# A four-layer graph network: layer 3's sums by accumulating DMAs, row spreads through DRAM, a new preparation

## The chip, the cores and the metric

The kernel runs on one NeuronCore of a Trainium2 chip. The time is device microseconds of one execution; the median of three runs is given. Engines: TensorE (PE, matrix products and transposes), VectorE (DVE), ScalarE (ACT), GpSimd (POOL), SyncE (SP, which issues DMAs; GpSimd and ScalarE can issue DMAs too). SBUF is the working memory of 128 partitions, PSUM the 8 banks that TensorE writes.

## The reference

32 samples of 512 nodes with 256 features pass through four layers; each adds its result to `x`. All share one 512 x 512 adjacency matrix `adj`. Everything is float32.

```python
h = max(layernorm(x), 0)                       # ahead of each layer
# layer 0: masked attention, 4 heads of 64
scores = q k^T / 8;  attn = softmax(where(adj == 0, -inf, scores));  x += concat(attn v) wo^T + bo
# layer 1: two graph attentions (GAT); the first without a mask, 512 features; the second masked, 256 features
gat(inp) = elu(softmax_j(leaky_relu(f1[i] + f2[j])) @ (inp W))
out = relu(h W1 + b1); out = elu(gat(out)) + out; out = relu(out W2 + b2); out = elu(gat(out)) + out; x += relu(out)
# layer 2: GAT with 4 heads of 64, masked;  x += elu(softmax_j(leaky(e_src[i] + e_dst[j])) @ q)
# layer 3: GAT with 8 heads of 32, masked, with beta*log(adj + 1e-6) added to the scores;  x += concat(...) W_out^T
```

The softmax is divided out late: the kernel forms the numerators `exp(score) * mask` for a block of 128 keys by 512 queries, multiplies them by the values, forms the sums over the keys apart, and divides afterwards.

## The kernel before, in words

**Preparation.** Lines 404 to 600 load the weights and `adj`, transpose `adj`, build the masks (`mask0T`, `mask1T`, `mask1`, `mask3T`), fold the attention vectors into the weight matrices (`w2`, `w3`, `fr1a`, `wh`) and compute a flag `go`, which says whether scores are small enough for the fast path. `go` is read by every engine as a branch; only the fast path, `pipelined`, runs here. `general` is the other branch. Preparation uses its own pool, `prep`; the tiles of `pipelined` come from the pool `big`, which takes the same memory once `prep` is freed.

**The planner.** `pipelined` writes no instruction directly. Each call through `q` is recorded as a step with an engine, a cost (function `cost`), the tiles it touches and its predecessors. When all 32 samples are recorded, `Plan.order` builds one order for all engines: it takes the step with the earliest start, and among those the one with the smallest due time. Due times come from `PERIOD` and the length of the chain behind a step, moved by `URGENT` for named tiles of a layer; `STARTS`, `PACE` and `LAYERS` hold samples and layers back. The steps are then issued in that order from line 261, so every operation of the pipeline has line 261 in the profile and is told apart by its tiles. Several samples are in flight, and each engine and each DMA queue runs its own part of the order strictly in sequence. The tiles of 128 x 512 share one tag, `block`, with `BLOCKS` buffers; PSUM tiles share the 8 banks.

**Units.** Products that use 32 or 64 columns (or 64 rows) of TensorE are issued in groups that fill the array; `unit("columns", ...)` or `unit("rows", ...)` marks such a group, with a packing mode that differs from full products.

**Layer 3 and layer 2** (`separable`, lines 889 to 943). Four heads at a time, the row `R[s]` of each head is spread over 128 partitions by a DMA from DRAM. For each of the 4 key blocks `j`, ScalarE and VectorE make four blocks `p` (one per head) and TensorE adds their products with the values to `av`. The sums over the keys are formed in two ways: in the first group of heads (`g == 0`; the only one of layer 2) VectorE adds the four `p` of each head into `total`, and TensorE multiplies the totals by ones at the end; in the second group of layer 3 TensorE multiplies every `p` by ones, into `sm`, in the same unit as `av`. Layer 3 then divides in `normalise` (lines 688 to 710): `sums` goes to DRAM, comes back as `few` (128 x 16), is inverted, goes to DRAM again, and comes back spread as `rc`. Layer 2 (lines 945 to 968) instead copies `av` and `sm` out as `y3`, transposes all three, and divides in node-major form.

**Layer 1** (`first_gat`, `second_gat`). The scores of the nodes come from the products `f1p`; a second product with `pick` brings them to node-major form. Three rows (`r1`, `rc`, `fb`) are spread over all partitions by four transposes each of a column broadcast to 128 x 128.

**The norm** (`norm_t`, lines 628 to 652) of every layer: statistics on VectorE, `rs` (a power of -0.5) on GpSimd, `h` on ScalarE, and eight transposes `pt` on TensorE.

Of the kernel before, what the change touches and what calls it, by code (L numbers as in the profile page):

```python
# [11 lines left out]
F32 = mybir.dt.float32  # L12
BF16 = mybir.dt.bfloat16
I32 = mybir.dt.int32
AF = mybir.ActivationFunctionType
# [15 lines left out]
G = 2  # L31
# [10 lines left out]
PERIOD = 51.0  # L42
STARTS, PACE = (0.0, 8.0, 36.0, 32.0), 110.0
LAYERS = (0.0, 51.0, 151.0, 201.0)

URGENT = {
    "stats:0": 76, "h:0": 358, "mm:0": 3, "sc:0": 60, "p0:0": -99, "av:0": 39, "stats:1": -269, "pt:1": 119,
    "nd:1": -201, "total:1": 12, "av:1": -22, "e:1": -39, "o2:1": 73, "s:1": -189, "pt:2": 15, "e4:2": -44,
    "total:2": 10, "stats:3": -38, "mv:3": -56, "mm:3": -12, "p3:3": -178, "total:3": -169, "sm:3": 86,
    "s1:3": -16,  # L50
}
BLOCKS, KEEP = 60, 2
KEEP_BANKS = 0
BANKS = ("mm", "av", "sm", "sc", "pt", "fb", "f1p")
# [242 lines left out]
def cost(engine, op, args, kw, out):  # L297
# [22 lines left out]
    if engine == "POOL":  # L320
        return (1.0 if n < 16 else 0.683), 0.1
    size = 4
    for _, k in (out.ap if out.tensor.name.startswith(("few", "R", "rc", "x")) else src.ap):
        size *= k
# [4 lines left out]
def gnn_stack_kernel(ctx: ExitStack, tc: tile.TileContext, a: dict, out: bass.AP):  # L329
# [29 lines left out]
    def load_col(name, eng):  # L359

        src = a[name]
        t = const.tile([P, src.shape[0] // P], F32, name=name)
        eng.dma_start(t, T(src, "(k p) -> p k", p=P))
        return t

# [19 lines left out]
    bq8 = const.tile([P, KD], F32, name="bq8")  # L385

# [6 lines left out]
    pick = const.tile([P, 2], F32, name="pick")  # L393
# [9 lines left out]

    prep_stack = ExitStack()
    prep = prep_stack.enter_context(tc.tile_pool(name="prep", bufs=2))
    pp = prep_stack.enter_context(tc.tile_pool(name="prep_psum", bufs=1, space=PSUM))
    with prep_stack, tc.manual_schedule():

        adj = prep.tile([P, NT, N], I32, name="adj", bufs=1)
        nc.gpsimd.dma_start(adj, T(a["adj"], "(t p) j -> p t j", p=P))  # L410
# [3 lines left out]
        nc.sync.dma_start(a2, bass.AP(tensor=src.tensor, offset=src.offset, ap=[[0, P], [1, 2 * F2]]))  # L414
        s3 = load_bcast(prep, "L3_a_src", nc.sync, D)
        d3 = load_bcast(prep, "L3_a_dst", nc.sync, D)
        wq = load_rows("wqT", nc.scalar, D)
        rows = []
        for name in ("bq", "bk"):
            t = prep.tile([1, D], F32, name=f"{name}r")  # L420
            nc.sync.dma_start(t, a[name][None, :])
            rows.append(t)
        for k in range(KD):
            nc.scalar.dma_start(
                T(w3[:, k, H3 : H3 + D], "p (h f) -> p h f", h=H3), T(a["L3_W"][:, k * P : (k + 1) * P, :], "h p f -> p h f")
            )
        wk = load_rows("wkT", nc.scalar, D)
        bt = load_bcast(prep, "beta", nc.sync, 1)
        bq = load_col("bq", nc.sync)
        bk = load_col("bk", nc.sync)  # L430
        afc = load_bcast(prep, "a_fc", nc.sync, 2 * HID)
        wo = load_rows("woT", nc.scalar, D)
        wv = load_rows("wvT", nc.scalar, D)
        wfc = load_rows("W_fc", nc.scalar, HID)
        bo = load_bcast(const, "bo", nc.sync, D)
        bv = load_bcast(const, "bv", nc.sync, D)
        bvc = prep.tile([P, KD], F32, name="bvc")
        nc.sync.dma_start(bvc, T(a["bv"], "(k p) -> p k", p=P))
        ahd = load_bcast(prep, "a_hand", nc.sync, 2 * D)
        b1 = load_col("mlp1_b", nc.sync)  # L440
        b2 = load_col("mlp2_b", nc.sync)
        wh = load_rows("W_hand", nc.scalar, D + 2)
        m1 = load_rows("mlp1_w", nc.scalar, HID)
        m2 = load_rows("mlp2_w", nc.scalar, D)
        w3o = load_rows("L3_WoT", nc.scalar, D)
# [10 lines left out]
        for c in range(2):  # L456
            nc.vector.tensor_reduce(pick[:, c : c + 1], ident[:, c:P:32], axis=AX.X, op=ALU.add)


        top = prep.tile([P, NT], F32, name="top")  # L460
        adjf = prep.tile([P, NT, N], F32, name="adjf", bufs=1)
        for t in range(NT):
            nc.vector.tensor_copy(adjf[:, t, :], adj[:, t, :])
        adjT = []
        for j in range(NT):
            pt = pp.tile([P, N], F32, name="adjT", bufs=NT)
            for t in range(NT):
                nc.tensor.transpose(pt[:, t * P : (t + 1) * P], adjf[:, t, j * P : (j + 1) * P], ident)
            adjT.append(pt)
        for t in range(NT):  # L470
            nc.vector.tensor_reduce(top[:, t : t + 1], adjf[:, t, :], axis=AX.X, op=ALU.max)
            nc.vector.tensor_scalar(mask1[:, t, :], adjf[:, t, :], 0.0, -BIG, op0=ALU.is_le, op1=ALU.mult)


        ab = prep.tile([P, 1], F32, name="ab")
        nc.vector.tensor_scalar(ab, bt, -1.0, None, op0=ALU.mult)
        nc.vector.tensor_tensor(ab, ab, bt, op=ALU.max)
        nc.scalar.activation(ab, ab, AF.Exp, scale=-1.0)
        m3 = [prep.tile([P, N], F32, name="m3", bufs=NT) for _ in range(NT)]
        for j in range(NT):  # L480
            nc.scalar.activation(m3[j], adjT[j], AF.Relu)
        nc.scalar.activation(ab, ab, AF.Ln, bias=one)

        ok = prep.tile([P, NT], F32, name="ok")
        nc.vector.tensor_scalar(ok, top, 0.0, None, op0=ALU.is_gt)
        nc.vector.tensor_scalar(top, top, 0.0, None, op0=ALU.max)
        nc.scalar.activation(top, top, AF.Ln, bias=eps)
        for j in range(NT):
            nc.scalar.activation(m3[j], m3[j], AF.Ln, bias=eps)
        nc.vector.scalar_tensor_tensor(beta, bt, 0.0, ab, op0=ALU.max, op1=ALU.add)  # L490

        for j in range(NT):
            nc.scalar.activation(m3[j], m3[j], AF.Exp, scale=beta)
# [9 lines left out]
        for w, h, f, vs, vd in (  # L503
            (w2, H2, F2, a2[:, 0:1, :].to_broadcast([P, H2, F2]), a2[:, 1:2, :].to_broadcast([P, H2, F2])),
            (w3, H3, F3, T(s3, "p (h f) -> p h f", h=H3), T(d3, "p (h f) -> p h f", h=H3)),
        ):
            project(lambda k: w[:, k, h : h + D], KD, h, f, vs, lambda k: w[:, k, :h])
            project(lambda k: w[:, k, h : h + D], KD, h, f, vd, lambda k: w[:, k, 3 * h + D :])
            nc.vector.tensor_scalar(w[:, :, h + D : 2 * h + D], w[:, :, :h], ALPHA - 1.0, None, op0=ALU.mult)
            nc.vector.tensor_scalar(w[:, :, 2 * h + D : 3 * h + D], w[:, :, 3 * h + D :], ALPHA, None, op0=ALU.mult)  # L510


# [3 lines left out]
        for w, row in zip((wq, wk), rows):  # L516
            gp = pp.tile([64, N], F32, name="gp", bufs=2)
            for h in range(4):
                c = slice(h * 64, (h + 1) * 64)
                for k in range(KD):  # L520
                    nc.tensor.matmul(gp[:, c], w[:, k, c], w[:, k, c], start=(k == 0), stop=False)
                nc.tensor.matmul(gp[:, c], row[:, c], row[:, c], start=False, stop=True)
# [10 lines left out]
        gab = prep.tile([64, D], F32, name="gab")  # L533
        nc.vector.tensor_copy(gab, gp[:, :D])
        nc.vector.tensor_tensor(gab, gab, gp[:, D:], op=ALU.mult)
        nc.vector.tensor_reduce(
# [865 lines left out]
```

## Time and profile before

| | |
|---|---|
| median of three runs | 4181.78 us (4181.32 to 4182.27) |
| the profiled execution's own time, and its span | 4184.13 us, 4182.3 us |
| TensorE busy | 4059.5 us, 97% |
| VectorE busy | 3312.1 us, 79% |
| ScalarE busy | 3004.7 us, 72% |
| GpSimd busy | 254.8 us, 6% |
| DMA moved | 181.07 MB; the hardware queue used 13.5% of 16 engines' span |
| granted TensorE clock, mean | 0.988 |
| additions into `total` (VectorE) | 832 and 416, 547.2 and 278.9 us |
| `sm<-p,ones` (TensorE, second group of layer 3) | 1024 records, 142.1 us |
| `y3` transposes (TensorE) | 384, 49.0 us |

A group's line gives the line and engine, the operation with the tiles written and read (buffer numbers left out), the shapes, the count, the busy time and the mean of one in ns, and after the bar the idle time of its engine just before it and what ended it. A timeline line gives the start, the duration, the engine, and how many like instructions were merged. The chain of work that ended last is followed back from the end of the execution. A float32 matrix product is two records, a transpose one. Durations of TensorE overlap; the distance of two starts is the time that one takes.

### The profile page before, as it was taken

What the parts mean: (1) busy time and instruction counts of PE and PEld (TensorE: products, weight loads), DVE (VectorE), ACT (ScalarE), POOL (GpSimd) and SP (SyncE); (2) the same over time, 40 slices, a digit from 0 to 9 for tenths busy, and PEclk for the clock granted to TensorE, in tenths of its full rate; (3) what the DMA queues carried; (4) which work ended last, traced back from release to release, by engine and by line L of the source; (5) the groups of instructions that cost most, each with busy time, mean ns of one, the idle gap of its engine ahead of it and who ended that gap; (6) DMA issues with size and microseconds to landing.
All of it is one profiled execution on the core that took longest, in us unless ns stands there. A gap on an engine that the chain in (4) does not pass through costs nothing.

```text
span 4182.3 us, 52787 instructions
## 1 busy us (share of the span) xinstructions
PE 4059.5 (97%) x17862; PEld 2068.7 (49%) x17862; DVE 3312.1 (79%) x7018; ACT 3004.7 (72%) x5970; POOL 254.8 (6%) x263
## 2 busy tenths in 40 slices
PE   5999999999999999999999999999999999999986
PEld 3545454554454554455554455554455554455442
DVE  5388877878877878877879877879877878877876
ACT  3467777766777766777766777776777776787774
POOL 1000000000000000000000000000000000000000
PEclk7999999999999999999999999999999999999998
DMA  2001111111110111110111111111111111111111
GB/s 84 11 21 47 47 47 33 49 52 32 47 51 30 49 52 32 47 52 30 49 52 32 47 52 31 47 52 32 47 52 32 46 52 32 47 52 32 41 42 52
DMA packets 149435, 181.07 MB, mean 43 GB/s; under 512 B 45858, under 2 KB 81572, under 8 KB 149156
## 3 DMA queue, kind: packets, MB, share of 16 engines
q1 hardware_dynamic: 143572, 172.37, 13.5%
q10 hardware_dynamic: 5312, 4.20, 0.3%
q8 instruction: 143, 2.34, 0.2%
q14 instruction: 136, 1.11, 0.1%
q0 software_dynamic: 272, 1.05, 0.1%
HBM read 158.41 MB, written 19.14 MB: 42 GB/s over the span
## 4 chain that ended last, share of the span: by engine, by line
PE 78%; DVE 13%; DMA 4%; ACT 2%; issue 1%; SPq 0%; POOL 0%; DVEq 0%; POOLq 0%
PE mm L261 36%; PE av L261 26%; PE pt L261 6%; PE sc L261 5%; PE sm L261 4%; DVE p L261 3%; DVE total L261 3%; DVE ue L261 2%; DMA rc<-s 2%; DVE o L261 2%; PE f1p L261 1%; DVE oT L261 1%; ACT p L261 1%; DVE x L261 1%; DMA s<-few 1%; DMA R<-rd 1%
## 5 line engine op out<-in xcount | busy, mean ns | idle before, releaser
L261 ACT ACTIVATE p<-R,e 128x512 f32<-128x512 f32 x1536 | 1010.2, 721 | 167.7 <-DMA R<-rd 167.5
L261 DVE SCALAR_TENSOR_TENSOR p<-p,e,mask3T 128x512 f32<-128x512 f32 x1024 | 718.2, 745 | 368.1 <-ACT p L261 367.9
L261 PE MATMUL av<-p,v 128*64 128x512 f32 (+1 forms) x2048 | 689.8, 597 | 1.4 <-DVE p L261 1.4
L261 DVE TENSOR_TENSOR total<-total,p 128x512 f32<-128x512 f32 x832 | 547.2, 680 | 0.0
L261 PE MATMUL av<-p,vs 128*32 128x512 f32 (+1 forms) x3072 | 524.8, 598 | 19.2 <-DVE p L261 19.1
L261 PE MATMUL mm<-W_fc,o 128*128 128x512 f32 x1024 | 467.0, 593 | 0.0
L261 PEld LDWEIGHTS av<-p,v 128*64 128x64 f32 (+1 forms) x2048 | 257.5, 163 | 363.4 <-issue 297.1
L261 POOL TENSOR_TENSOR rs<-ve,mhalf 128x4 f32<-128x4 f32 x128 | 151.0, 1180 | 3764.2 <-DVE ve L261 3593.1
L261 DVE SCALAR_TENSOR_TENSOR p<-p,e,mask1T 128x512 f32<-128x512 f32 x512 | 367.6, 742 | 5.8 <-ACT p L261 5.4
L261 ACT ACTIVATE h<-x,ms,rs 128x256 f32<-128x256 f32 x512 | 269.7, 593 | 128.7 <-DVE ms L261 128.7
L261 DVE TENSOR_TENSOR p<-p,mask0T 128x512 f32<-128x512 f32 x512 | 324.1, 681 | 38.3 <-ACT p L261 38.3
L261 PEld LDWEIGHTS av<-p,vs 128*32 128x32 f32 (+1 forms) x3072 | 135.8, 119 | 346.0 <-issue 239.0
L261 PEld LDWEIGHTS mm<-W_fc,o 128*128 128x128 f32 x1024 | 188.9, 190 | 210.0 <-issue 183.4
L261 DVE TENSOR_TENSOR total<-p,p 128x512 f32<-128x512 f32 x416 | 278.9, 678 | 1.0
L261 ACT ACTIVATE p<-sc 128x512 f32<-128x512 f32 x512 | 262.9, 687 | 7.7 <-PE sc L261 7.7
L261 PE MATMUL mm<-w,hT 128*128 128x272 f32 (+1 forms) x1024 | 262.3, 398 | 1.8 <-ACT hT L261 1.8
L261 PE MATMUL av<-pT,v 128*128 128x512 f32 x512 | 239.9, 593 | 0.5 <-ACT pT L261 0.4
L261 PE MATMUL mm<-o,mlp_w 128*128 128x512 f32 x512 | 228.8, 598 | 0.0
L261 PE MATMUL sc<-qT,kT 64*128 64x512 f32 x1024 | 228.3, 595 | 0.0
L261 PE MATMUL mm<-hT,mlp_w 128*128 128x512 f32 x512 | 225.7, 592 | 0.0
L261 PEld LDWEIGHTS mm<-w,hT 128*128 128x128 f32 x1024 | 188.1, 193 | 54.8 <-ACT hT L261 10.3
L261 ACT COPY sums<-sm 128x512 f32<-128x512 f32 x96 | 55.8, 581 | 195.8 <-PE sm L261 195.7
(187 smaller groups left out, 6076.5 us busy)
## 6 DMA issues: line engine op xcount, KB each, us to landing
R<-rd SPq DMA_DIRECT2D x384, 256.0 KB
x<-in_x_dram SPq DMA_DIRECT2D x32, 512.0 KB
rc<-s SPq DMA_DIRECT2D x128, 128.0 KB
rc<-s SPq DMA_DIRECT2D x256, 64.0 KB
out_dram<-x SPq DMA_DIRECT2D x32, 512.0 KB
s<-sums SPq DMA_DIRECT2D x96, 8.0 KB
few<-s SPq DMA_DIRECT2D x96, 8.0 KB
s<-few SPq DMA_DIRECT2D x96, 8.0 KB
```

The source lines that it names most:

```text
L261: getattr(getattr(self.nc, attribute), op)(*args, **kw)
```

## The change

- Layer 3, both head groups: `total` is gone. The `p` blocks of key blocks 1 to 3 are added into the `p` of key block 0 (`first`) by DMAs with an accumulating write, issued by GpSimd. TensorE forms the sums with one unit at the end of each group. Layer 2 keeps VectorE's additions.
- Layer 2 divides in `normalise`, as layers 0 and 3 do, before the transposes; its end works on two node blocks at a time.
- Layer 1: a new `spread` turns the columns with one transpose, copies 4 x 128, and spreads the row over DRAM with two DMAs issued by GpSimd. It makes `r1`, `rc` and `fb`. The products with `pick` become four transposes and a VectorE reduction.
- `rT` of layers 2 and 3: one transpose of 16 or 32 columns instead of four; the scores are copied in two pieces.
- Preparation: other queues and another order; `adj` in four DMAs from SP; the biases arrive as rows and are turned by TensorE; ScalarE copies the transposed adjacency out of PSUM; `mask1` is made after `go`. `x` comes from a pool, `first`, that does not wait for `prep`.
- The planner's constants are new, and `BLOCKS` goes from 60 to 59. `cost` gets a value for a DMA that GpSimd issues.

```diff
-PERIOD = 51.0
-STARTS, PACE = (0.0, 8.0, 36.0, 32.0), 110.0
-LAYERS = (0.0, 51.0, 151.0, 201.0)
+PERIOD = 48.0
+STARTS, PACE = (0.0, 4.0, 26.0, 107.0), 74.0
+LAYERS = (0.0, 6.0, 205.0, 267.0)
...
-BLOCKS, KEEP = 60, 2
+BLOCKS, KEEP = 59, 2
...
+        if op == "dma_start":
+            return 1.1, 3.3
...
+    first = ctx.enter_context(tc.tile_pool(name="first", bufs=1))
...
-        nc.gpsimd.dma_start(adj, T(a["adj"], "(t p) j -> p t j", p=P))
+        for t in range(NT):
+            nc.sync.dma_start(adj[:, t, :], av[:, t, :])
...
+        def spread(name, cols):
+            pt, few = bank("pt"), q.tile(big, [P, P], "turned", 4)
+            q.tensor.transpose(pt[:NT, :P], cols, ident)
+            q.scalar.copy(few[:NT, :], pt[:NT, :P])
+            row = q.tile(dram, [NT, P], "row", 8)
+            q.gpsimd.dma_start(row, few[:NT, :])
+            b = block(name)
+            q.gpsimd.dma_start(b, T(row, "t p -> (t p)")[None, :].to_broadcast([P, N]))
+            return b
...
-            f1p = bank("f1p")
-            for t in range(NT):
-                q.tensor.matmul(f1p[:, 2 * t : 2 * t + 2], part[:, col(t)], pick, start=True, stop=True)
-            q.vector.tensor_copy(T(sd, "p t c -> p (t c)"), f1p[:, : 2 * NT])
+            pt = bank("pt")
+            for t in range(NT):
+                q.tensor.transpose(pt[:, col(t)], part[:, col(t)], ident)
+            q.vector.tensor_reduce(sd, T(pt, "p (t k c) -> p t c k", k=KH, c=32)[:, :, :2, :], axis=AX.X, op=ALU.add)
...
-            pt = bank("pt")
-            for t in range(NT):
-                q.tensor.transpose(pt[:, col(t)], ew[:, 2, t : t + 1].to_broadcast([P, P]), ident)
-            r = block("r1")
-            q.scalar.copy(r, pt)
+            r = spread("r1", ew[:, 2, :])
...
-                q.tensor.transpose(fb[:, col(t)], v[:, t, D + 1 : D + 2].to_broadcast([P, P]), ident)
+            fb = spread("fb", v[:, :, D + 1])
...
-            for t in range(NT):
-                q.tensor.transpose(pt[:nh, col(t)], e[:, t, :nh], ident)
-            rT = block("rT")
-            q.scalar.copy(rT[:nh, :], pt[:nh, :])
+            q.tensor.transpose(pt[: NT * nh, :P], es, ident)
+            rT = q.tile(big, [P, P], "rT", 4, tag="turned")
+            q.scalar.copy(rT[: NT * nh, :], pt[: NT * nh, :P])
...
-                        if added and j:
+                        if j and total:
                             q.vector.tensor_tensor(total[s], first[s] if j == 1 else total[s], p[s], op=ALU.add)
-                    if added and not j:
+                        elif j:
+                            q.gpsimd.dma_start(out=first[s], in_=p[s], accum_op=ALU.add)
+                    if not j:
                         first = p
                     st = dict(start=(j == 0), stop=(j == NT - 1))
-                    with q.unit("columns", (0.86 if per == 4 else 1.72) + (0 if added else 0.86)):
+                    with q.unit("columns", 0.86 if per == 4 else 1.72):
...
-                        if not added:
-                            for s in range(4):
-                                q.tensor.matmul(sm[s * F3 : (s + 1) * F3, :], ones[:, :F3], p[s], **st)
...
+                sm = bank("sm")
+                with q.unit("columns", 0.86):
+                    for s, b in enumerate(total or first):
+                        q.tensor.matmul(sm[s * F3 : (s + 1) * F3, :], ones[:, :F3], b, start=True, stop=True)
...
-                for b, ps in zip(y, avs + [sm]):
-                    q.scalar.copy(b, ps)
+                y.extend(normalise(avs, sm))
...
-                for k in range(3):
-                    q.tensor.transpose(pt[:, col(k)], y[k][:, col(t)], ident)
+                for i in range(2):
+                    for k in range(KD):
+                        q.tensor.transpose(pt[:, col(2 * i + k)], y[k][:, col(t + i)], ident)
...
-            xt = q.tile(big, [P, NT, D], "x", 4)
+            xt = q.tile(first, [P, NT, D], "x", 4)
```

## The prediction

> **What bounds the kernel now.** I read the page's engine totals, then busy time by stretch, then TensorE's timeline in one steady stretch, then the groups, the last chain and the preparation.
>
> The totals name a candidate:
>
> ```profile
> PE 4059.5 (97%) x17862; PEld 2068.7 (49%) x17862; DVE 3312.1 (79%) x7018; ACT 3004.7 (72%) x5970; POOL 254.8 (6%) x263
> ```
>
> By stretch (TensorE, weight loads, VectorE, ScalarE, GpSimd, then granted clock, DMA share and GB/s), TensorE works 497.46 of 500 us in the middle, and 228.55 of 283 at the end:
>
> ```profile
> 60.00:120.00 60.00, 53.88 (x215) 25.78 (x216) 36.84 (x86) 36.31 (x70) 16.36 (x20) 0.91 0.12 39
> 2000.00:2500.00 500.00, 497.46 (x2220) 254.75 (x2218) 409.43 (x865) 372.85 (x744) 31.55 (x32) 1.00 0.14 43
> 3900.00:4183.00 283.00, 228.55 (x935) 107.44 (x931) 195.46 (x403) 171.26 (x339) 8.25 (x6) 0.91 0.14 44
> ```
>
> Output stores leave every 125.2 us there, which is one sample: TensorE 124.6 us, VectorE 102.5 (82%), ScalarE 93.3 (75%). So work taken from TensorE counts one to one; work taken from the others only widens their margin.
>
> Starts, not the overlapping durations, price TensorE's work (a matrix product is two records):
>
> ```profile
> 2092.47 1.04 PE L261 MATMUL sm<-p,ones 128*32 128x512 f32 x8
> 2093.33 1.04 PE L261 MATMUL av<-p,vs 128*32 128x512 f32 x8
> ...
> 2111.74 0.95 PE L261 MATMUL f1p<-pick,part 128*128 128x2 f32 x8
> 2112.55 0.68 PE L261 MATMUL mm<-L_WoT,oT 128*128 128x256 f32 x2
> ...
> 2117.79 0.60 PE L261 MATMUL pt<-ident,ew 128*128 128x128 f32 x4
> 2118.23 0.60 PE L261 MATMUL mm<-L_WoT,oT 128*128 128x256 f32 x2
> ```
>
> A quad of 32-column products takes 0.86 us, four tiny products with `pick` 0.81, a transpose 0.11. From one packing mode to another the next start comes 0.11 to 0.19 us later than these prices.
>
> **The change, part by part.** The sum is against the profiled execution: span 4182.3 us, own time 4184.1; the median of the runs is 4181.8, 0.5 below the span. The span splits into 65.6 us before the first transpose of sample 0, 4042.6 us of TensorE work after it (4059.5 less 16.9 in preparation) and 74 us of TensorE idle: 54 after 3900 us, 20 before.
>
> *TensorE, per sample.* Layer 3's second head group forms its sums in one quad, not four: 3 x 0.86 = 2.58. Transposes: layer 2's end 12 to 8; `r1`, `rc`, `fb` and both `rT` 4 to 1 each: 19 x 0.11 = 2.09. The `pick` products become four transposes: 0.81 - 0.44 = 0.37. Together 5.04 us, x32 = 161 us. The new order switches packing mode 13.1 times a sample instead of 9.5; 3.6 x 0.15 x 32 = 17 us back (no lower than 13; up to 33 if all of the 2.7 us by which 124.6 exceeds the priced sum of 121.9 is switching, 0.29 each). All of it is on the path.
>
> *VectorE.* Layer 3's first group loses 12 additions a sample:
>
> ```profile
> L261 DVE TENSOR_TENSOR total<-total,p 128x512 f32<-128x512 f32 x832 | 547.2, 680 | 0.0
> L261 DVE TENSOR_TENSOR total<-p,p 128x512 f32<-128x512 f32 x416 | 278.9, 678 | 1.0
> ```
>
> They are 12 of 39: 826.1 x 12/39 = 254 us, 7.9 a sample. Layer 2's end goes from 16 small operations (5.5 us) to a reciprocal, two products and four 512-wide operations (4.5). About 93.5 of 120 us remain, 78%: beside other work, counted at nothing. ScalarE trades wide copies of `rT`, `r1`, `rc` for narrow ones and for 8 more small score copies: about even, again 78%.
>
> *The accumulating DMAs.* 24 a sample, 256 KB each, on GpSimd's queue, plus 6 for the spread rows; GpSimd goes from 8 to 38 instructions a sample and SP from 37 to 44 (7 x 0.42 = 3 us, beside other work). GpSimd's one DMA before, and the quiet landing of 256 KB rows:
>
> ```profile
> 1.31 0.92 POOL L410 DMA_DIRECT2D adj<-in_adj_dram  x1 [0.36 <-issue]
> ...
> 4124.27 3.66 SPq L261 DMA_DIRECT2D R<-rd  x8
> ...
> 4127.85 2.08 ACT L261 ACTIVATE p<-R,e 128x512 f32<-128x512 f32 x3 [5.11 <-DMA R<-rd]
> ```
>
> Issue: 0.92 us (for 1 MB, so hardly more for 256 KB), x30 = 28 us of GpSimd, plus 4 `pow` of 1.18 and 4 additions of 0.80: 35 of 120 us. Landing: no row has an accumulation; a load is used 3.6 us after its issue, and reading both operands could double that: 3.6 to 7.2. I take 3.6, the row of the same size. DMA share: 172 MB took 13.5%; 201 MB more, read twice, add 16 to 32% of the shorter span. What hides it is the order: in three groups of four, 36 us of TensorE work stand between the point by which the last key block must be ready and the sums that need it. In the fourth the bound is only 4.6 us, so 7.2 would cost up to 2.6 us every second sample, 42 us; at the low end nothing. A wait there holds whatever follows on GpSimd's queue: `rs` of the next norm and the spread rows.
>
> The Trainium skill's DMA: Bandwidth & Descriptors (Anatomy of one DMA) gives a DMA from GpSimd about 2.0 us plus bytes over 436 GB/s, by which an estimate for 256 KB is 2.6 us; the sum would stay as it is, since no wait appears. Against the change speaks SBUF — State Buffer (Who interferes with whom): VectorE's two-port modes lock GpSimd out while it writes descriptors. `p<-r,ew` takes 542 ns where other forms of that size take 680; if that is such a mode, four a sample would hold GpSimd 2.2 us, an estimate of 69 us over the run if all of it reached TensorE, and no row before can show it.
>
> *Longer chains.* Layer 2's normalisation now makes the round trip through DRAM that the last chain shows: sums done 4115.03, product 4124.97, 9.9 us.
>
> ```profile
> 4115.67 1.66 DMA s<-sums
> ...
> 4117.35 1.62 DMA few<-s
> ...
> 4119.27 1.40 DMA s<-few
> ...
> 4121.98 2.06 DMA rc<-s
> ...
> 4124.97 3.97 PE mm L261 x10
> ```
>
> In the new order 11.9 to 14.1 us of TensorE work cover it: 2 to 4 to spare. A spread row (narrow copy 0.3, two issues 1.8, two landings 1.6 and 3.1, `p` 0.5) is 7.3 us under 11.4 at the tightest. A norm from the last addition to its first transpose is 4.7 to 6.0 us (4.0 in the preparation's rows from statistics to transpose) under 7.3 to 12.9; before, those covers were 10.8 to 24.4, and TensorE idled 0.5%. If a DMA is late, the next sample's transposes and all TensorE work behind them wait. I take 0.6 us a sample, 19 us; ends 0 (covers hold) and 4 us, 128 us (each of four chains late by 1 us).
>
> *Preparation.* ScalarE starts late because it issues loads; `x` waits for the pool to be freed:
>
> ```profile
> 24.75 1.28 ACT L478 ACT_TABLE_LOAD   x1 [24.75 <-DMA mlp_b<-in_mlp_b_dram]
> ...
> 61.53 1.41 DVE L261 BATCH_NORM_STATS2 stats<-x 128x6 f32<-128x256 f32 x4 [4.29 <-DMA x<-in_x_dram]
> ```
>
> VectorE is busy 30.6 of the first 60 us. The new order leaves ScalarE few loads and lets `x` load at the branch: the 4.3 us wait goes, and the branch value, at 42.9 now, needs the adjacency (11.5), about 15 us of VectorE work and TensorE round trips: some 28 to 33. Bounds: 4 us (weights late) to 20; 1.7 us of `mask1` moves behind the branch. I take 15.6.
>
> Sum: 4182.3 - 15.6 - 161 + 17 + 19 = 4042; as a median **4041 us**.
>
> **The rivals.**
> - *The new chains wait (slower than forecast, still faster).* For: covers shrank to 2 to 4 us while the DMA share doubles, and each chain now has up to four DMAs. Against: three of four sums have 36 us. At 2.5 to 4 us a sample rather than 0.6: 4041 + 32 x (1.9 to 3.4) = 4102 to 4150.
> - *The accumulating DMA becomes the bound (slower than before).* Place: GpSimd's queue, 24 a sample behind each other. With 13.4 us a sample for its other work, GpSimd passes 125.2 us when one accumulation costs it 4.7 us of issue or of waiting; at 5.0 the sample takes 133.4 us and the run 4182 + 32 x 8.2 = 4444. Against: the row of 0.92 us and the loads' 3.6 us, which overlap; for: no row prices an accumulation.
> - *The gain is not there.* If VectorE or ScalarE decided the pace, only the preparation would be left: 4166. Against: 82% and 75% beside TensorE's 99.5%.
> - *Covers hold and the preparation gives its best.* 4041 - 19 - 5 = 4017, or 3995 with a shorter end, where VectorE loses its additions.
>
> **How the numbers follow.** Forecast (4000 to 4075, with the ends of preparation, switching and small waits): 0.60. Waiting chains up to 4175: 0.24. DMA-bound: 0.11. No gain: 0.03, half of it within 0.2% (8 us, about what this measurement can tell). Better than 4000: 0.02. The range 3995 to 4160 leaves out the slow rival, the far part of the waiting one and little below. Faster 0.87, within 0.2% 0.02, slower 0.11.
>
> **What would show it.** Right: stores 120 to 121 us apart, TensorE over 98% busy in the middle, no `sm<-p` inside the loop over key blocks, about 0.9 us per DMA issue on GpSimd, first transpose near 50 us, VectorE near 3050 us. Wrong: TensorE's idle before `sm` put down to an accumulation, before transposes of `h` to `rs`, or before layer 2's transposes to `rc`; GpSimd busy over 60%; ScalarE waiting for `p` blocks to be freed.

## The result and the profile after

| | before | after |
|---|---|---|
| median, us (lowest to highest) | 4181.55 (4180.15 to 4182.27) | 4426.82 (4423.55 to 4431.92) |
| span of the profiled execution | 4182.3 | 4424.3 |
| first transpose of sample 0 | 65.6 | 51.5 |
| TensorE busy after it, and idle after it | 4042.6, 74 | 4016.7, 356 |
| output stores apart, in the middle | 125.2 | 132.9 on average (130.0 to 136.3 from 1200 to 3870 us) |
| granted TensorE clock, mean | 0.988 | 0.955 |

The ratio of after to before is 1.0588 (95% interval 1.057 to 1.0606): slower by 5.9%, where 3.4% faster was forecast.

The page of after: engine totals, the two large DMA queues (packets, MB, share of all 16 DMA engines), and the accumulating DMA with its size and its median time from issue to landing.

```profile
PE 4039.8 (91%) x16382; PEld 2007.1 (45%) x16382; DVE 3084.9 (70%) x6345; ACT 2955.3 (67%) x6198; POOL 1030.7 (23%) x1224
...
q0 software_dynamic: 121440, 227.02, 29.2%
q1 hardware_dynamic: 165402, 194.07, 14.0%
...
p<-p POOLq DMA_DIRECT2D x768, 256.0 KB, 9.6
```

TensorE's work did fall, but it is busy for only 91% of a longer span. VectorE and ScalarE have more room than before (70 and 67% for 79 and 72%), and GpSimd, up from 6%, is busy for 23%. So no engine has become the bound. An accumulation lands 9.6 us after its issue, where the forecast took 3.6 and held 7.2 for the worst.

The same stretches as before, by busy time (the last three columns are granted clock, DMA share, GB/s):

```profile
2000.00:2500.00 500.00, 462.32 (x1904) 229.28 (x1904) 360.66 (x731) 346.67 (x735) 124.62 (x148) 0.96 0.47 102
3900.00:4425.00 525.00, 414.66 (x1598) 189.87 (x1596) 321.66 (x630) 302.90 (x636) 133.73 (x153) 0.89 0.51 107
```

In the middle TensorE now stands idle for 38 of 500 us, and its clock is down from 1.00 to 0.96. What it waits for is in the groups, first two of before, then those of after:

```profile
L261 ACT ACTIVATE p<-R,e 128x512 f32<-128x512 f32 x1536 | 1010.2, 721 | 167.7 <-DMA R<-rd 167.5
L261 PE MATMUL av<-p,v 128*64 128x512 f32 (+1 forms) x2048 | 689.8, 597 | 1.4 <-DVE p L261 1.4
```

```profile
L261 ACT ACTIVATE p<-R,e 128x512 f32<-128x512 f32 x1536 | 1012.2, 734 | 333.0 <-DMA R<-rd 262.4 <-DMA p<-p 69.9 <-DVE p L261 0.3
L261 PE MATMUL av<-p,v 128*64 128x512 f32 (+1 forms) x2048 | 747.6, 628 | 226.0 <-DVE p L261 226.0
...
L261 PE MATMUL sm<-p,ones 128*32 128x512 f32 x512 | 74.3, 621 | 13.1 <-DMA p<-p 13.1
```

226 us of idle stand before `av<-p,v`, where before had 1.4: 27 waits of 4.8 to 9.8 us, 8.4 on average, one in nearly every sample. They are waits for VectorE's `p` and belong to layer 1. The place where one would look for a slow accumulation, the sums `sm<-p,ones` that read its result, lost only 13.1 us in the whole run. And ScalarE waits 262 us for `R`, whose own load the change left as it was (only `rT`, from which it comes, is made differently). In before it waited 167 us there too, but at most 5.9 us at a time, and TensorE felt nothing of it; now single waits reach 12.9 us.

**One sample, step by step.** GpSimd's timeline of after (start, duration, instructions merged, and in brackets its idle time and what ended it):

```profile
2039.70 1.39 POOL L261 TENSOR_TENSOR rs<-ve,mhalf 128x4 f32<-128x4 f32 x1 [22.09 <-DVE ve L261]
2041.40 12.61 POOL L261 DMA_DIRECT2D p<-p  x14 [0.32 <-PE av L261]
...
2057.52 2.67 POOL L261 DMA_DIRECT2D p<-p  x3
...
2065.97 4.43 POOL L261 DMA_DIRECT2D p<-p  x5
```

An accumulation writes into the `p` of key block 0, which TensorE has to read first. VectorE had the first `p` of this group ready by 2019, TensorE reads them from 2040 on; from then on 14 accumulations are free at once, and GpSimd issues them in 12.6 us, 0.9 us each. That is not GpSimd's limit: it is idle again afterwards. What the DMA engines make of it is in stretches of 4 us (the DMA share is the time of all packets that start in the stretch, over 16 engines, and can pass 1):

```profile
2040.00:2044.00 4.00, 4.00 (x44) 1.24 (x40) 3.02 (x6) 4.00 (x9) 3.69 (x6) 1.00 0.31 53
2048.00:2052.00 4.00, 4.00 (x20) 1.87 (x16) 3.94 (x7) 4.00 (x10) 4.00 (x6) 1.00 1.11 181
...
2064.00:2068.00 4.00, 3.68 (x21) 0.72 (x16) 4.00 (x7) 0.58 (x1) 2.58 (x5) 1.00 1.12 191
...
2072.00:2076.00 4.00, 0.00 (x0) 0.00 (x0) 0.00 (x0) 0.00 (x0) 0.00 (x0) 0.66 1.10 236
2076.00:2080.00 4.00, 0.96 (x1) 0.50 (x2) 2.31 (x5) 3.07 (x6) 0.00 (x0) 0.50 0.90 242
2080.00:2084.00 4.00, 4.00 (x7) 1.67 (x6) 4.00 (x7) 4.00 (x8) 0.00 (x0) 0.56 0.07 19
```

The DMA share is full from 2044 to nearly 2080. The queue of accumulations and spread rows used 29.2% of 4424.3 us, 1292 us of all 16 engines together; without accumulations the same queue uses 90 us (2.1% of 4286.4 us, experiment 4). The difference over 768 is 1.56 us of all 16 engines for one accumulation, and 23 of them issued from 2041.4 on need 36 us: until 2077. In this stretch layer 2 of another sample asks for its rows. The timeline of after, first SP's queue, then ScalarE, VectorE and TensorE, shows who waits for whom:

```profile
2062.45 0.65 SPq L261 DMA_DIRECT2D rd<-rT  x1
2068.59 5.13 SPq L261 DMA_DIRECT2D R<-rd  x4
...
2076.93 0.72 ACT L261 ACTIVATE p<-R,e 128x512 f32<-128x512 f32 x1 [12.26 <-DMA R<-rd]
...
2077.69 0.75 DVE L261 SCALAR_TENSOR_TENSOR p<-p,e,mask1T 128x512 f32<-128x512 f32 x1 [8.98 <-ACT p L261]
2078.35 1.45 DVE L261 TENSOR_SCALAR p<-r,ew 128x512 f32<-128x512 f32 x3
...
2079.04 11.03 PE L261 MATMUL av<-p,v 128*128 128x512 f32 x20 [9.23 <-DVE p L261]
```

From `rd` issued to `R` issued takes 6.1 us. In before the same two lines of layer 2 stand 1.4 us apart:

```profile
1994.66 0.25 SPq L261 DMA_DIRECT2D rd<-rT  x1
1996.09 1.76 SPq L261 DMA_DIRECT2D R<-rd  x4
```

Over the 32 samples the median is 6.3 us in after and 1.4 in before. And from `R`'s issue to its first use it takes 8.3 us instead of 3.6. VectorE, whose order is fixed, stands 9 us at layer 2's `p`, which waits for this `R`; behind it stands layer 1's `p<-r,ew`, and TensorE's next work is the `av` of that `p`. After the wait TensorE's clock is granted at 0.50 to 0.56 for another 4 us and more (the rows of 2076 and 2080).

The burst has a second way to TensorE. An accumulation that lands late also keeps the `p` that it reads, and ScalarE has to wait for a free buffer:

```profile
ACT p L261 <- DMA p<-p: 107.0, 58, 11.9
```

That is 107.0 us in 58 waits, the longest 11.9; before had none. 37 us of them stand before layer 0's `p<-sc`, behind which come VectorE's `total` and TensorE's `sm<-total,ones`.

### The profile page after: what moved, and what is told of

It is laid out like the page before. It is cut to its first block, busy times and chain, and to the rows that moved or that the text cites. A ratio compares the mean times of both kernels' runs of the same rounds, so it can differ in the third digit from the quotient of the medians.

```text
span 4424.3 us, 52615 instructions
## 1 busy us (share of the span) xinstructions
PE 4039.8 (91%) x16382; PEld 2007.1 (45%) x16382; DVE 3084.9 (70%) x6345; ACT 2955.3 (67%) x6198; POOL 1030.7 (23%) x1224
## 3 DMA queue, kind: packets, MB, share of 16 engines
q0 software_dynamic: 121440, 227.02, 29.2%
## 5 line engine op out<-in xcount | busy, mean ns | idle before, releaser
L261 PE MATMUL av<-p,v 128*64 128x512 f32 (+1 forms) x2048 | 747.6, 628 | 226.0 <-DVE p L261 226.0
L261 POOL DMA_DIRECT2D p<-p x768 | 682.5, 1781 | 317.4 <-DVE p L261 176.5
L261 PEld LDWEIGHTS av<-p,v 128*64 128x64 f32 (+1 forms) x2048 | 280.3, 175 | 626.9 <-issue 316.7
L261 DVE SCALAR_TENSOR_TENSOR p<-p,e,mask1T 128x512 f32<-128x512 f32 x512 | 353.8, 743 | 248.1 <-ACT p L261 248.1
L261 PE MATMUL av<-p,vs 128*32 128x512 f32 (+1 forms) x3072 | 501.1, 597 | 8.8 <-DVE p L261 7.8
L261 DVE TENSOR_TENSOR total<-total,p 128x512 f32<-128x512 f32 x576 | 362.7, 682 | 0.1
L261 POOL DMA_DIRECT2D row<-turned x96 | 52.9, 551 | 1094.5 <-ACT turned L261 1027.3
L261 ACT ACTIVATE e<-y 128x512 f32<-128x512 f32 x128 | 80.9, 634 | 285.7 <-DVE y L261 285.3
L261 DVE TENSOR_TENSOR oT<-raw,rc 128x512 f32<-128x512 f32 x192 | 132.2, 690 | 192.0 <-DMA rc<-s 190.3
L261 PE MATMUL sc<-qT,kT 64*128 64x512 f32 x1024 | 239.8, 604 | 0.7 <-ACT v L261 0.7
```

The source lines that it names most:

```text
L261: getattr(getattr(self.nc, attribute), op)(*args, **kw)
```

## The experiments

**The theory:** the accumulations fill the 16 DMA engines for 35 us at a stretch; `R` comes late; VectorE's queue hands the delay to layer 1, TensorE stands idle and loses its clock. **The rivals:** GpSimd's queue, which issues 24 DMAs a sample where it issued none; the longer chains of the rest of the change (layer 2's normalisation, spread rows, norms); and the new order as such. Where a kernel's lines of the planner grew, the pipeline's line is 270 or 277 instead of 261.

### 1 and 2: the same DMAs, fewer bytes

The first leaves out half of each addition, the second seven eighths.

```diff
-q.gpsimd.dma_start(out=first[s], in_=p[s], accum_op=ALU.add)
+q.gpsimd.dma_start(out=first[s][:, :256], in_=p[s][:, :256], accum_op=ALU.add)   # e1_half
+q.gpsimd.dma_start(out=first[s][:, :64], in_=p[s][:, :64], accum_op=ALU.add)     # e2_eighth
```

> The changed kernel with one edit: the accumulating DMAs add only the first 256 of 512 columns (it leaves out half of each addition, so the sums of layer 3 are incomplete). The order, the number of DMA issues and every wait stay the same; only the bytes halve. Theory (the DMA engines are full for some 34 us of each sample, because 24 accumulations of 1.58 us each come in one burst; the spread rows R then land 12 us late, VectorE waits in order, and TensorE stands 9.3 us before layer 1's products): engine time of the accumulations 38 -> 19 us a sample, TensorE's wait falls from 9.3 to 0 to 3 us, the time to 4060 to 4200 us. Rival (GpSimd's queue: the issues themselves and the waits behind which r1 stands): nothing changes, 4380 to 4430 us.

> The same with 64 of 512 columns (seven eighths of each addition are left out): 128 rows of 256 B. Theory: no stretch with full DMA engines is left apart from the loads of R, and the sum of the prediction without its waits is reached: 4020 to 4080 us. Rival (GpSimd's queue): 4380 to 4430 us. If e1 is fast and this is no faster, 19 us a sample were already hidden.

Measured: half 4144.61 us, ratio 0.9912 (0.9896 to 0.9929); an eighth 4062.22 us, 0.9712 (0.9696 to 0.9728), both in the theory's ranges. All instructions, waits and the order are those of after. The page of the kernel with an eighth, and its stretch in the middle:

```profile
PE 3934.8 (97%) x16382; PEld 1974.8 (49%) x16382; DVE 3073.8 (76%) x6345; ACT 2945.7 (72%) x6198; POOL 1032.3 (25%) x1224
...
L261 ACT ACTIVATE p<-R,e 128x512 f32<-128x512 f32 x1536 | 1010.0, 738 | 45.5 <-DMA R<-rd 45.4
...
L261 PE MATMUL av<-p,v 128*64 128x512 f32 (+1 forms) x2048 | 688.9, 596 | 8.1 <-DVE p L261 7.3
```

```profile
2000.00:2500.00 500.00, 497.27 (x2075) 249.58 (x2074) 392.66 (x799) 381.34 (x802) 130.37 (x154) 1.00 0.26 61
```

GpSimd is as busy as in after (1032 us); there too it issues 14 accumulations in 12.5 us. But ScalarE's wait for `R` goes from 262 over 102 (half) to 45 us, and the idle time before `av<-p,v` from 226 over 58 to 8. ScalarE's waits for buffers held by accumulations are gone in both. With an eighth `R` is issued 2.0 us after `rd` (median), with `rT` made as in after, so the new `rT` is not what delays it. The stores are 121.2 us apart on average (120.0 to 123.0), close to the 120 to 121 forecast. So the bytes decide, and GpSimd's queue does not. The step from full to half gives 282 us, from half to an eighth 82: the cost grows faster than the bytes.

### 3: the same bytes, copied

```diff
-q.gpsimd.dma_start(out=first[s], in_=p[s], accum_op=ALU.add)
+q.gpsimd.dma_start(out=first[s], in_=p[s])
...
-nc.vector.tensor_tensor(mask3T[:, j, :], m3[j], mask1T[:, j, :], op=ALU.mult)
+nc.vector.tensor_tensor(mask3T[:, j, :], m3[j], mask1T[:, j, :], op=ALU.max)
```

> The changed kernel with plain copies in place of the accumulations: p overwrites first with the same 256 KB, issues, order and waits (the sums of layer 3 are then those of the last key block alone; the mask of layer 3 keeps small positive values so that no sum is zero). If the second operand that an accumulation reads is what fills the DMA engines, a copy takes 0.8 instead of 1.58 us and the time is as with half the bytes, 4060 to 4200 us. If the bytes written or the descriptors are what counts, 4380 to 4430 us.

Measured: 4171.07 us, 0.9979 (0.997 to 0.9989), 256 us less than with the accumulating write, and in the range given for a cheaper copy. Its page:

```profile
q0 software_dynamic: 72288, 227.02, 15.5%
...
p<-p POOLq DMA_DIRECT2D x768, 256.0 KB, 4.4
```

The megabytes are the same, the packets 72288 instead of 121440, and the engine time of one DMA is (15.5% of 4168.4 less 90) / 768 = 0.72 us instead of 1.56. Per byte the accumulating write costs the DMA engines 2.2 times a plain one. One thing does not fit: the copy has less engine time than half-width accumulations (0.91 us each) and is yet 0.6% slower, with ScalarE's wait for `R` at 120 us against 102. Engine time is not the whole price. The copies also come faster: GpSimd is busy 410.7 us for 768 of them, 0.53 us each, where accumulations take 0.89 (682.5 us). So copies are issued closer together than their 0.72 us of engine time, and half-width accumulations hardly are (0.89 and 0.91); whether that is the reason is not shown.

### 4: the rest of the change, without accumulations

```diff
-total = blocks("total", 4) if nh == H2 else None
+added = g == 0
+total = blocks("total", 4) if added else None
+if not added:
+    sm = bank("sm")
...
-elif j:
-    q.gpsimd.dma_start(out=first[s], in_=p[s], accum_op=ALU.add)
...
+if not added:
+    for s in range(4):
+        q.tensor.matmul(sm[s * F3 : (s + 1) * F3, :], ones[:, :F3], p[s], **st)
```

> The changed kernel with layer 3's sums formed as before (VectorE adds in the first head group, TensorE multiplies every block by ones in the second); all else as changed, planned anew with the changed constants. Theory: the rest of the change is sound: TensorE keeps 2.46 of the 5.04 us a sample, 79 us, and the preparation 14 us: 4080 to 4130 us. Rival (the row spreads and layer 2's round trip through DRAM are what waits): slower than before, 4200 to 4350 us.

Measured: 4286.06 us, 1.0246 (1.0228 to 1.0263): in the rival's range. The idle times lie elsewhere (before `mm<-L_WoT` 38.8 us, before `mm<-woT` 24.9; 57.6 of it waiting for VectorE's `oT`). But this kernel is ordered by a planner whose constants belong to another mix of steps, so it tells two causes in one. The same kernel with the constants searched again (`PERIOD`, `STARTS`, `PACE`, `LAYERS`, `URGENT`; the code is that of the diff above):

> The same kernel as e4_noacc (layer 3's sums as before: VectorE's additions in the first head group, 1024 products with ones on TensorE in the second; no accumulating DMA; layer 2's normalisation through DRAM, the spread rows and the preparation as changed), but with the planner's constants searched again for this mix, so that its order is not one made for other costs. Theory (the accumulations alone cost the time, the rest of the change gains what was forecast): the forecast's sum without the 2.58 us of sums per sample, 4182 - 16 (preparation) - 79 (2.46 us of transposes and pick x32) + 17 (packing modes) + 19 (small waits) = 4123; 4090 to 4160. Rival (the longer chains of layer 2 and the spread rows lose as well; then the 4286 of e4_noacc was not the order's fault): above 4200.

Measured: 4151.24 us, 0.9922 (0.9905 to 0.9938), within the theory's range. Its page and its middle:

```profile
PE 4030.7 (97%) x17150; PEld 2011.5 (48%) x17150; DVE 3295.9 (79%) x6729; ACT 2936.0 (71%) x6198; POOL 367.6 (9%) x456
...
L261 ACT ACTIVATE p<-R,e 128x512 f32<-128x512 f32 x1536 | 1018.2, 742 | 33.2 <-DMA R<-rd 32.6
```

```profile
2000.00:2500.00 500.00, 499.84 (x2157) 250.98 (x2158) 416.21 (x842) 363.84 (x773) 47.00 (x58) 1.00 0.19 56
```

TensorE is busy 499.84 of 500 us. Layer 2's trip through DRAM, the spread rows, the single transposes and the preparation cost TensorE no idle time worth naming in the middle; what made 4286 out of this kernel was the order. It is the fastest kernel here that computes everything, and beats both.

### 5: the additions on GpSimd itself

```diff
-q.gpsimd.dma_start(out=first[s], in_=p[s], accum_op=ALU.add)
+q.gpsimd.tensor_tensor(first[s], first[s], p[s], op=ALU.add)
...
-if op == "dma_start":
+if op == "dma_start" or n == N:
```

> The changed kernel with GpSimd adding the blocks itself (24 additions of 128 x 512 a sample) in place of issuing accumulating DMAs; the planner is given the same cost for it, so the order of TensorE, VectorE, ScalarE and SyncE is the same. It takes the 38 us a sample of DMA time away and leaves the 24 places on GpSimd's queue. By the row of x<-x,boa (0.74 us for 256 columns) an addition takes about 1.5 us, 36 us a sample, 49 of 120 with the rest. Theory (DMA engines full, R late): the wait before layer 1's products goes, 4040 to 4110 us. Rival (GpSimd's queue is what delays r1 and the norms): 4300 us or more, since each place on that queue gets longer, 1.5 instead of 0.9 us. If additions on GpSimd slow VectorE's own two-operand operations, VectorE's busy time rises above 3085 us and the time lies between.

Measured: 4847.7 us, 1.159 (1.1571 to 1.1609), the slowest of all. That is above the theory's 4110 and inside the open range of the rival (4300 or more), but by the third way that was named: the wait for `R` did go (24.2 us), while VectorE's busy time rose from 3085 to 3857 us. Groups of this kernel:

```profile
L261 POOL TENSOR_TENSOR p<-p,p 128x512 f32<-128x512 f32 x768 | 1151.5, 1533 | 267.2 <-DVE p L261 209.0 <-PE av L261 48.4 <-DVE mv L261 4.1
...
L261 DVE SCALAR_TENSOR_TENSOR p<-p,e,mask3T 128x512 f32<-128x512 f32 x1024 | 1013.8, 1042 | 206.2 <-ACT p L261 206.0
L261 DVE TENSOR_TENSOR p<-p,mask0T 128x512 f32<-128x512 f32 x512 | 741.7, 1503 | 83.6 <-ACT p L261 83.6
```

In after, the last two take 749 and 680 ns. The Trainium skill's SBUF — State Buffer (Who interferes with whom) says that a VectorE instruction with two inputs in SBUF contends with a GpSimd instruction that reads SBUF. Both of these have two such inputs, and the trace agrees: the 163 `mask0T` products that overlap an addition in time took 3.27 us on average, the other 349 0.68; of the `mask3T` products 342 took 1.63 us and the other 682 0.75. As a test of the theory the run is of little use: it removed one wait and made a larger one.

### 6: the preparation alone

Before, with the new preparation (loads on other queues, `adj` in four DMAs, biases as rows, `mask1` behind `go`) and the pool `first` for `x`, and nothing else.

```diff
+first = ctx.enter_context(tc.tile_pool(name="first", bufs=1))
...
-nc.gpsimd.dma_start(adj, T(a["adj"], "(t p) j -> p t j", p=P))
+for t in range(NT):
+    nc.sync.dma_start(adj[:, t, :], av[:, t, :])
```

> The kernel before with the new preparation and the new pool of x alone; pipeline and planner as before. Every theory: the first transpose moves from 65.6 to about 51 us and the end with it, 4163 to 4172 us. If the first layers are then held by late weights, less than that: 4172 to 4182.

Measured: 4168.63 us, 0.9967 (0.9955 to 0.998). The first transpose comes at 50.8 us, and the time falls by 13.5 us: this part gives nearly the 15.6 that were forecast.

### 7: layer 1 ahead of layer 2 in VectorE's queue

```diff
-            for step in self.order():
+            for step in self.ahead(self.order()):
```

`ahead` puts a `p1` step (layer 1's `p<-r,ew`) in front of the `p3` step of layer 2, of another sample, that stands just before it on VectorE.

> The changed kernel in full, with all its transfers; only VectorE's order is altered: in the planned order, layer 1's products p1 (p<-r,ew) are put ahead of the layer 2 products p3 (p<-p,e,mask) of the other sample that stand just before them on VectorE and that wait for R. Theory (the accumulations' burst delays R; layer 2's p waits for R at the head of VectorE's in-order queue, and layer 1's p1, whose r landed some 5 us earlier, stands behind it; TensorE's idle time before layer 1's av is that queue): the idle time of TensorE before av<-p,v falls from 9.3 to about 3 us per sample, 27 times some 6 us, and some of the clock comes back: 4170 to 4260 us. R itself stays as late as it was (ACT p waiting for R about 12 us each). Rival A (r itself lands late, or what comes behind layer 2's p is late next, so that the wait only changes its place): 4380 to 4430 us. Rival B (the lower granted clock and not the wait is the cause): the waits go, the clock stays at 0.955 and the time at 4330 to 4400 us.

Measured: 4370.66 us, 1.045 (1.0432 to 1.0467); idle before `av<-p,v` between 500 and 3800 us 132 instead of 202 us. The time is between the theory's and rival A's. It lies in rival B's range, but B's condition, that the waits go and the low clock alone remains, is not met: two thirds of the wait are still there. The timeline says why (GpSimd, VectorE, ScalarE, TensorE of this kernel):

```profile
2046.06 0.57 POOL L277 DMA_DIRECT2D r<-row  x1 [3.70 <-PE av L277]
...
2052.45 1.46 DVE L277 TENSOR_SCALAR p<-r,ew 128x512 f32<-128x512 f32 x3 [3.08 <-DMA r<-row]
2053.14 9.57 PE L277 MATMUL av<-p,v 128*128 128x512 f32 x18 [2.68 <-DVE p L277]
2056.91 0.72 ACT L277 ACTIVATE p<-R,e 128x512 f32<-128x512 f32 x1 [11.60 <-DMA R<-rd]
...
2063.61 0.54 DVE L277 TENSOR_SCALAR p<-r,ew 128x512 f32<-128x512 f32 x1
...
2064.20 1.12 PE L277 MATMUL av<-p,v 128*128 128x512 f32 x2 [1.48 <-DVE p L277]
```

Layer 1's `p<-r,ew` no longer waits for `R`, and TensorE's wait of 9.2 us became 2.7. But `r` itself, 256 KB spread by the same queue, now lands 6.4 us after its issue (4.9 with an eighth of the bytes, 3.6 without accumulations), and the fourth `p<-r,ew` still has layer 2's products ahead of it. So VectorE's queue was about a third of this wait (70 of 202 us); the rest is rows that come late. The theory had the place right and the share wrong. Total idle after the first transpose fell from 356 to 278 us, the time by only 56: TensorE was busy 24 us longer, with its clock, at 0.963, hardly back; short waits of 1 to 3 us cost clock too (0.62 to 0.83 in single stretches of 4 us here).

### 8: a planner that knows the price

```diff
+            if step.wire:
+                wire = max(wire, start + step.busy + 1.0) + step.wire
+                end = max(end, wire + 1.0)
...
+            step.wire = 1.57 if "accum_op" in kw else n / 313e3
```

> The changed kernel in full, all 768 accumulations of 256 KB, re-planned: the planner now holds the 16 DMA engines as one shared resource, on which an accumulation takes 1.57 us and any other DMA its bytes at 313 GB/s, and its constants are searched again for that. Theory (the time is lost because the order was made for transfers that do not delay each other, and the burst of 24 x 1.57 = 38 us collides with R's loads): with the collision in the plan the waits move to where something covers them; TensorE's idle time before layer 1's av falls from 9 us a sample to under 4, 4130 to 4300 us. Rival (38 us of full DMA engines in a sample of 125 us can't be placed, whatever the order): 4350 to 4450. Accumulations' landing stays 7 to 10 us under either.

Measured: 4254.32 us, 1.0172 (1.0155 to 1.0189), in the theory's range, 173 us better than after with all 768 accumulations in it. Groups and landing on its page:

```profile
L270 ACT ACTIVATE p<-R,e 128x512 f32<-128x512 f32 x1536 | 998.2, 725 | 116.4 <-DMA R<-rd 114.5
...
L270 PE MATMUL av<-p,v 128*64 128x512 f32 (+1 forms) x2048 | 692.6, 596 | 0.0
...
p<-p POOLq DMA_DIRECT2D x768, 256.0 KB, 7.7
```

The wait before `av<-p,v` is gone. The rest is spread thin (82 us of idle between 500 and 3700, clock 0.972 over the run, stores 127 us apart on average), and the kernel stays slower than before. So much of the loss was the order's. How much of the 173 us comes from the plan's knowledge of the DMA engines and how much from searching its constants again is not shown: experiment 4 gained 135 us by a new search alone. No order found here makes 24 accumulations a sample pay.

### 9 and 10: accumulations in one of the two groups

```diff
-total = blocks("total", 4) if nh == H2 else None
+total = blocks("total", 4) if g == 0 else None
```

> The changed kernel, but only layer 3's second head group is summed by accumulating DMAs (12 a sample, 384 in all); the first group's additions are VectorE's again, as before the change. Constants searched again for this mix, with 1.6 us of issue and 5.0 us to landing for an accumulation. TensorE has all of the gain of the forecast. Theory: the burst is at most 12 x 1.57 = 19 us, as long in DMA time as with half-width accumulations (4145 us in e1_half) and without the order's fault for it; VectorE's 7.9 us a sample come back (about 100 of 122). 4070 to 4170, faster than before. Rival (any burst beside R's loads loses what TensorE gains): 4180 to 4300.

> The same mix as e6t_onegroup, planned instead with the DMA engines as one shared resource (1.57 us for an accumulation) and constants searched for that. If the collision in the DMA engines is what counts, this order is at least as good as that of e6t_onegroup: 4060 to 4170. If VectorE's and GpSimd's queues count instead, the plan's own end, which is 1.4% later than that of e6t_onegroup, decides, and it is 1 to 2% slower than e6t_onegroup.

Measured: 4233.34 us, 1.0116 (1.0098 to 1.0133), in the rival's range; and, with the DMA engines in the plan, 4173.49 us, 0.9975 (0.9965 to 0.9985), a little over the theory's 4170. The waits of the first and of the second (total, times, longest):

```profile
DVE oT L261 <- DMA rc<-s: 139.6, 110, 6.7
ACT p L261 <- DMA R<-rd: 48.8, 65, 5.3
```

```profile
DVE oT L270 <- DMA rc<-s: 29.8, 38, 5.1
ACT p L270 <- DMA R<-rd: 24.1, 12, 5.3
```

The same steps, two orders, 60 us apart; the plan that ends 1.4% later by its own count is 1.4% faster on the chip, and waits far less for the normalisation's and `R`'s loads. That these now keep out of the accumulations' way fits it, but the two orders differ everywhere. Nor does the faster one reach the 4151 of the kernel without accumulations. Whether half of them could pay stays open: with 768 fewer products TensorE is busy 4034.0 us against 4030.7 there, and 73 us of that stand in `sm<-total,ones` (179.7 against 107.0), whose products start one by one as VectorE's totals come in. The waits do not put that down to the accumulations: ScalarE waited 24.1 us for `R` and 1.4 for buffers that they held.

## Why the prediction was wrong

**The step that failed** is the price of an accumulating DMA: "Landing: ... I take 3.6, the row of the same size", and beside it a DMA share that would "add 16 to 32% of the shorter span", taken as an average. The average was right, the queue's share is 29%; but the landing was read off loads on quiet engines. The runs show 1.56 us of all 16 DMA engines for one accumulation, 2.2 times a copy's 0.72; 0.9 us between issues; so a queue builds up by itself, and landing is 9.6 us. In the forecast's sum this stands in the last term, TensorE's idle time of 74 + 19 = 93 us, which came out at 356.

**The second half of the same step** is "What hides it is the order". It asked who waits for the accumulations' result, and that cover held: 13.1 us before `sm<-p`. It did not ask what the landing holds up elsewhere: ScalarE's 107 us of waiting for buffers is the forecast's own sign of being wrong, "ScalarE waiting for `p` blocks to be freed". And it did not ask who shares the 16 engines with them, though the forecast's own rows had it: `R` is 256 KB four at a time. The Trainium skill's SBUF — State Buffer ("Can I just issue two DMAs to hit both halves?") says that all of a kernel's DMAs land on the same 16 engines, whoever issues them; the runs agree, with `R` used 8.3 us after its issue beside the burst and 3.6 without it. The estimate of 2.6 us for 256 KB that the forecast worked out from DMA: Bandwidth & Descriptors (Anatomy of one DMA) stands against 9.6 us here, 4.4 for a copy, and 4.2 even for 32 KB; none of these rows is from quiet engines.

By the forecast's terms, 4426.8 against 4041:

| term | forecast | measured | difference |
|---|---|---|---|
| start, to the first transpose | 50 | 51.5 | +1.5 |
| TensorE's work after it (4042.6 - 161 + 17) | 3898.6 | 4016.7 | +118 |
| idle after it (74 + 19) | 93 | 356 | +263 |
| median against span | -0.5 | +2.5 | +3 |

Idle: 226 of the 356 us are the wait before `av<-p,v`. Busy: after stands 105 us above the kernel with an eighth of the bytes (4016.7 against 3911.7), 59 of it in `av<-p,v`, which follows the wait at half the granted clock, and 28 in `sm<-total,ones` (98.1 against 69.9 us). There one product is as short as with an eighth (608 and 606 ns); the products start apart, as their totals come in, and such short pauses count as busy. The other 13 of the 118 us are there with an eighth of the bytes too. So the clock that a wait costs is a term of its own, some 59 us to 226 us of waiting, and the forecast had none for it. The Trainium skill's TensorE: Matmul & The Clock Gate (Part 1: The HAM clock gate) states that the clock is halved after an idle window of about 3.4 us; the rows of 0.50 and 0.56 behind the 9.2 us wait agree with it. But shorter waits were enough too. With half the bytes, TensorE's line and the stretch behind it read:

```profile
2583.57 8.80 PE L261 MATMUL av<-p,v 128*128 128x512 f32 x16 [2.07 <-DVE p L261]
```

```profile
2585.00:2588.00 3.00, 3.00 (x5) 1.30 (x4) 3.00 (x5) 3.00 (x6) 0.00 (x0) 0.50 0.17 29
```

Of the 23 waits of 1.9 to 2.6 us in that run (500 to 3800 us), 15 were followed by 3.4 us at half clock; of those from 0.7 to 1.5 us none was.

**What held.** With an eighth of the bytes the kernel is at 4062, 21 us from the forecast: start 51.4, TensorE 3911.7, idle 100.6, stores 121.2 us apart. Without accumulations the same terms gave 4123 and the run 4151: TensorE 24 more than the 3981 forecast, idle 93 as forecast, the start 3 later. So transposes, packing modes, preparation (13.5 of 15.6), layer 2's normalisation and the spread rows add up to within 1% of the run's time; but for the preparation none of them was measured alone. GpSimd's issue was 0.89 us for 0.92, VectorE 3085 us for 3050.

**The rivals.** "The accumulating DMA becomes the bound" gave 4444, 0.4% from the result, but by GpSimd's queue, which issues as much and as densely in the kernel with an eighth of the bytes at 4062. Its number was right by chance: the bound is not a queue that issues, but the engines behind it, and these for 35 us of each sample only. "The new chains wait" named the doubled DMA share as its reason; it looked in the changed chains, and the wait came at `R`, which it did not name. The fear of VectorE's two-port modes holding up GpSimd's issue (69 us at worst) was hardly put to the test: issue stayed at 0.89 us, but only 5 of the 768 accumulations overlapped a `p<-r,ew` in time.

## What to carry to other kernels

Price a DMA by what it takes of the shared DMA engines as well as by its landing, and lay this against the burst in which it is issued, not against the span: 24 x 1.56 us is 28% of a sample of 133 us on average, and 100% for 35 us. Then ask which loads of other stages fall in that burst, and who stands behind the instruction that waits for them in an in-order queue. When an order comes from a planner, a kernel with one part undone needs its constants searched again before its time says anything of that part (4286 against 4151 here).

## What the hardware showed that was not expected

- An accumulating DMA in SBUF takes 1.56 us of all 16 DMA engines for 256 KB, 0.91 for 128 KB and 0.41 for 32 KB (19.1% of 4142.7 us and 9.9% of 4063.6 us, each less 90 us, over 768); a plain copy of 256 KB takes 0.72, with 60% of the packets. By the packet records of the traces an accumulation moves its data in 128 packets of 2 KB, 188 ns each at the median; the copy in 64 packets of 4 KB, 172 ns each.
- GpSimd's issue time does not depend on the size: 14 accumulations take 12.6 us at 256 KB and 12.5 us at 32 KB. It does depend on the kind: 0.89 us for an accumulation, 0.53 for a copy of the same size.
- TensorE's granted clock fell to a half after every wait of 4.8 us or more in after (25 from 500 to 3800 us), and after 15 of 23 waits of 1.9 to 2.6 us with half the bytes.
- GpSimd's additions of 128 x 512 take 1.53 us each and slow VectorE's products with two SBUF inputs from 680 to 1503 ns and from 749 to 1042 ns, which cost this kernel more than the DMAs did (4848 us against 4427).
